# Three steps of a first attention's loop moved between engines and units: the halves of the sums, the weight pieces' rescaling, and the division

## The chip, the cores and the metric

The kernel runs on one core of one Trainium2 chip. A core has five engines that run their own instruction streams and wait for each other by semaphores: TensorE (PE; its weight loads are shown as PEld), VectorE (DVE), ScalarE (ACT), GpSimd (POOL) and SyncE (SP), which here issues all DMAs. The metric is the time of one execution on the device in microseconds; the kernel before has a median of 2089.02 us over 10 runs (2085.13 to 2091.97).

## The reference, cut to what matters

Two layers, each a cross attention, a second mixing stage and a feed-forward part, work on x of 16 batches x 64 tokens x 512 features. The change lies in the first cross attention, over a context of 1601 tokens of 256 features per batch, and in a weight preparation for the last feed-forward part that runs beside it:

```python
qh = (q @ Wq + bq).reshape(B, LQ, HEADS, D_K).transpose(0, 2, 1, 3)   # 16 heads of 32
kh = (k @ Wk + bk)...;  vh = (v @ Wv + bv)...
attn = jax.nn.softmax(jnp.einsum('bhqd,bhkd->bhqk', qh, kh) / np.sqrt(D_K), axis=-1)
out = jnp.einsum('bhqk,bhkd->bhqd', attn, vh)          # then concat @ Wo + bo, added to x
...
s = jnp.maximum(jnp.max(jnp.abs(wb), axis=-1, keepdims=True) / qmax, 1e-12)   # blocks of 32 weights, qmax = 7
wq = jnp.clip(jnp.round(wb / s), -qmax - 1.0, qmax) * s
```

So for each head and query the kernel needs a maximum over the keys, exponentials, their sum, the product with the values, and a division by the sum; and each block of 32 weights of the last feed-forward part is divided by a scale, rounded, and multiplied by the scale again.

## The kernel before, in words

All data are float32. The first attention is a loop over 33 rounds, `for u in range(U + 1)` (L416), with U = 32 units; a unit is one batch and half of the heads (8 heads, 64 queries: 512 columns). Keys lie on partitions, in KC = 13 chunks of 128 (the last has 65). Round u does the first half of unit u (projections of keys and values, scores, running maximum) and the second half of unit u - 1 (subtracting the maximum, exponentials, sums, attention, division). The order within each engine is the order of the text: each instruction of the loop goes through `pin = tc.keep_in_program_order`. DMAs go to SP's queue.

What a round does, with the lines:

- `diagonal(u)` (L273): four POOL copies of the queries into a zeroed tile. For u below 8, POOL also adds a bias to x (L436).
- `next_k` / `k_proj` (L201 by way of `pmm`, L215): keys of unit u, eight pairs of matmuls into the PSUM pool `ps_mm` of two buffers, taken out by ACT. Among them stand `maxima(u - 1)` (L292 transposes `mt`, L294 reduction on DVE) and `shift(u - 1)` (L301 transposes `nb`, L307: seven DVE additions of the negated maximum onto the scores).
- `next_exps` / `exps(u - 1, k)` (L315 on ACT, two chunks at a time). POOL adds the pairs of chunks into `acc`, which has two halves (L320, then L322 four times); with the last, single chunk it adds the second half of `acc` onto the first (L324) and then the last chunk (L325).
- `piece_round(u - 1)` (L169): DVE rounds a piece of weights (L171), POOL multiplies it by its scales (L172), SP stores it (L173). `piece_load(u)` (L156, L160) then loads the next piece. The tiles of a piece (`w`, `wsc`, `winv`) have two buffers.
- `next_v` / `v_proj` (L201, L226): a chunk of values, two matmuls into `ps_mm`, and a DVE addition that takes it out of PSUM; a third chunk needs a buffer that the first one's addition frees. Between them stand `scores(u, 0..2)` (L201; L261 and L265 on ACT) and, on DVE, `running_max(u, k)` (L281, L283, L286).
- In every fourth round (u = 5, 9, ..., 29) `project(g)` (L201, L358) multiplies a finished block of 128 tokens by the output weights; in some rounds a block is normalised and transposed for the next stage.
- The tail: the last two pairs of value chunks before it end, then DVE does `running_max` 4 and 6, `piece_scale(u)` (L164, L165, L166 on DVE, L167 on POOL), `running_max` 8 and 10, two value additions, `running_max` 12, the fold of the two halves of the maximum (L491) and the last value addition. PE meanwhile does `scores(u, 2)`, `attend(u - 1)` (208 matmuls into `av`), `sum_up(u - 1)` (eight matmuls of ones with `acc`) and the value chunks 10, 11, 12. SP issues `load_ctx` in odd rounds (L189).
- `divide(u - 1)` (L349 reciprocal, L350 product, both on DVE, out of the PSUM tile `av`, which has one buffer) ends the round.

Pieces 0 to 30 are prepared in this loop, the other five in the feed-forward stage of the first layer (L768 to L773).

Of the kernel before, what the change touches and what calls it, by code (L numbers as in the profile page):

```python
# [47 lines left out]
def perceiver_kernel(ctx: ExitStack, tc: tile.TileContext, x_d, ctxT_d, ctx_d, cols_d, rows_d,  # L48
# [107 lines left out]
    def piece_load(n, prep):  # L156
        w = prep.tile([P, 16, 32], F32, name="w", tag="wraw")
        raw[n] = (w, prep.tile([P, 16], F32, name="wsc", tag="wsc"),
                  prep.tile([P, 16], F32, name="winv", tag="winv"))
        nc.sync.dma_start(out=w, in_=pieces[n].rearrange("p (b i) -> p b i", b=16))  # L160

    def piece_scale(n, pin=free):
        w, sc, inv = raw[n]
        pin(v.tensor_reduce(sc, w, AX.X, ALU.max, apply_absolute_value=True))  # L164
        pin(v.tensor_scalar(sc, sc, 1.0 / 7.0, 1e-12, ALU.mult, ALU.max))  # L165
        pin(v.reciprocal(inv, sc))  # L166
        pin(gp.tensor_tensor(w, w, inv.unsqueeze(2).to_broadcast([P, 16, 32]), ALU.mult))  # L167

    def piece_round(n, pin=free):  # L169
        w, sc, inv = raw.pop(n)  # L170
        pin(v.tensor_scalar(w, w, RND, RND, ALU.add, ALU.subtract))  # L171
        pin(gp.tensor_tensor(w, w, sc.unsqueeze(2).to_broadcast([P, 16, 32]), ALU.mult))  # L172
        nc.sync.dma_start(out=grid[n], in_=w.rearrange("p b i -> p (b i)"))  # L173

# [3 lines left out]
    with ExitStack() as st1:  # L178
# [117 lines left out]
        def shift(u):  # L296


            nb = ps_mx.tile([P, 4, P], F32, name="nb", tag="mx")
            for j in range(4):  # L300
                pin(pe.transpose(nb[:, j, :], nms[u][:, j:j + 1].to_broadcast([P, P]), ident))  # L301
            nb = nb.rearrange("p j e -> p (j e)")
            f = flat(u)
            for k in range(0, KC, 2):
                n = min(2, KC - k)
                m = nkeys(k + n - 1)
                pin(v.tensor_tensor(f[:m, k:k + n, :], f[:m, k:k + n, :],  # L307
                                    nb[:m].unsqueeze(1).to_broadcast([m, n, 512]), ALU.add))

        def exps(u, k):  # L310

            n = min(2, KC - k)
            m = nkeys(k + n - 1)
            f = flat(u)
            pin(s.activation(f[:m, k:k + n, :], f[:m, k:k + n, :], AF.Exp))  # L315
            if u == 2 * B - 1:
                return
            if k == 2:
                accs[u] = mxp.tile([P, 2, 512], F32, name="acc", tag="acc")
                pin(gp.tensor_tensor(accs[u], f[:, 0:2, :], f[:, 2:4, :], ALU.add))  # L320
            elif 2 < k and n == 2:
                pin(gp.tensor_tensor(accs[u], accs[u], f[:, k:k + 2, :], ALU.add))  # L322
            elif n == 1:
                pin(gp.tensor_tensor(accs[u][:, 0], accs[u][:, 0], accs[u][:, 1], ALU.add))  # L324
                pin(gp.tensor_tensor(accs[u][:m, 0], accs[u][:m, 0], f[:m, k, :], ALU.add))  # L325

        def attend(u, i):
# [18 lines left out]
        def divide(u):  # L346
            b, hf = u // 2, u % 2
            rs = mxp.tile([P, 2, LQ], F32, name="rs", tag="rs")
            pin(v.reciprocal(rs, avs[u][:, 1]))  # L349
            pin(v.tensor_tensor(qo[:, 2 * hf:2 * hf + 2, b * LQ:(b + 1) * LQ], avs[u][:, 0], rs,  # L350
                                ALU.mult))
# [64 lines left out]
        for u in range(U + 1):  # L416
            old, new = u >= 1, u < U
            k_at = iter(range(0, KC, 2))

            def next_exps(n):  # L420
                for _ in range(n if old else 0):
                    exps(u - 1, next(k_at))

            def next_k(i, z):
                if old and new:
                    k_proj(u, i, z)

            def next_v(*ks):
                for k in ks:
                    if old or k >= EARLY:  # L430
                        v_proj(u, k)

            if new:
                diagonal(u)
            if u < G:
                pin(gp.tensor_tensor(x[:, u, :], x[:, u, :], row(R_BO0), ALU.add))  # L436

            normed = [(g, ln_norm(g, pin)) for g in NORM0.get(u, ())]
            next_k(0, 0)
            if old:  # L440
                maxima(u - 1)
            next_k(0, 1)
            if old:
                shift(u - 1)
            next_k(0, 2)
            for g, xn in normed:
                ln_transpose(g, xn, ps_mm, pin)
            next_k(0, 3)
            for z in range(4):
                next_k(1, z)  # L450
                next_exps((1, 1, 0, 2)[z])
            if not new:

                next_exps(3)
                attend(u - 1, 0)
                attend(u - 1, 1)
                sum_up(u - 1, [(flat(u - 1)[:, k, :], nkeys(k)) for k in range(KC)])
                divide(u - 1)
                break
            if old and u <= NPREP:  # L460
                piece_round(u - 1, pin)
            if u < NPREP:
                piece_load(u, prep)
            next_v(0, 1)
            scores(u, 0)
            next_exps(2)
            next_v(2, 3, 4, 5)
            running_max(u, 2)
            if u >= 2 and (u - 2) % 4 == 3:
                g = (u - 2) // 4  # L470
                project(g)
                ln_stats(g, pin)
                if g in (3, 6):
                    ln_scale(0 if g == 3 else 4, g + 1, pin)
            scores(u, 1)
            next_exps(1)
            next_v(6, 7, 8, 9)
            running_max(u, 4)
            running_max(u, 6)
            if u < NPREP:  # L480
                piece_scale(u, pin)
            scores(u, 2)
            if old:
                attend(u - 1, 0)
                attend(u - 1, 1)
                sum_up(u - 1, [(accs[u - 1][:, 0], P)])
            running_max(u, 8)
            running_max(u, 10)
            next_v(10, 11)
            running_max(u, 12)  # L490
            pin(v.tensor_tensor(rms[u][:, 0], rms[u][:, 0], rms[u][:, 1], ALU.max))  # L491
            next_v(12)
            if u % 2 and u // 2 + 2 < B:
                load_ctx(u // 2 + 2)
            if old:
                divide(u - 1)
        project(G - 1)
        ln_stats(G - 1)
        ln_scale(G - 1, G)
# [170 lines left out]
    with ExitStack() as st3:  # L670
# [78 lines left out]
        for q in range(2):  # L749
            t = slice(q * 512, (q + 1) * 512)  # L750
            hT = hp.tile([P, NBLK, 512], F32, name="hT", tag="hT")
            for i in range(NBLK):
                ps = ps3.tile([P, 512], F32, name="ps", tag="mm")
                for c in range(4):
                    mm(ps, w1[:, c, i * P:(i + 1) * P], xnT[:, c, t], c == 0, c == 3)
                s.activation(hT[:, i, :], ps, AF.Relu, bias=col(C_B1 + i))
                v.tensor_tensor(hT[:, i, :], hT[:, i, :], masks[16 * q + i - i % 2][:, i % 2, :],
                                ALU.mult)
                if i % 2:
                    load_mask(16 * q + i + 5)  # L760
                if q and i % 2 == 0 and 2 <= i < 10:
                    ln_out(i // 2 - 1, ps3)
                if not q and i == 1:
                    ln_out(G - 1, ps3)
                    add_rows(row(R_B2))
                if not q and i == 3:
                    route(1)
                if not q and 2 <= i < 2 + len(todo):  # L768
                    piece_load(todo[i - 2], prep)
                if not q and 3 <= i < 3 + len(todo):  # L770
                    piece_scale(todo[i - 3])
                if not q and 4 <= i < 4 + len(todo):
                    piece_round(todo[i - 4])  # L773
            if q:

                ffn0.close()
                ctxa = pool(early, "ctxa4", bufs=2, side="right")
                load_T(0)
            for k in range(4):
                g = 4 * q + k  # L780
                po = ps3.tile([P, 512], F32, name="ps", tag="mm")
                for i in range(NBLK):
                    mm(po, hT[:, i, k * P:(k + 1) * P], w2[:, i, :], i == 0, i == NBLK - 1)
                v.tensor_tensor(x[:, g, :], x[:, g, :], po, ALU.add)
                ln_stats(g)
                if g == 6:
                    ln_scale(4, 7)
            if q == 0:
                ln_scale(0, 4)
# [518 lines left out]
```

## Time and profile before

The profile is of one execution, taken by the hardware profiler.

| what | value |
|---|---|
| median of 10 runs | 2089.02 us |
| the profiled execution's own time | 2084.11 us |
| its span, first to last instruction | 2082.4 us |
| granted TensorE clock over the span | 0.988 |
| first attention's loop, first `av` matmul to last division | 107.6 to 1210.4 us |
| a unit, from one `nb` to the next | 34.6 to 38.4 us |
| busy of the span: PE, DVE, ACT, POOL | 94%, 58%, 38%, 38% |

How to read it: a row of the timeline has the start in us, the duration, the engine, the line, the operation, the tiles it writes and reads, the shapes and the number of instructions merged into the row. In brackets stands the idle time of the engine before it and what ended it. Durations of DVE and POOL contain any time that the instruction itself is held up after its start. The ends of matmuls are modelled.

### The profile page before, as it was taken

To read this page: it belongs to the slowest core of one execution; us is meant where nothing else is said; L and a number is where in the kernel's file an instruction comes from. 1 tells how busy PE (TensorE), PEld (TensorE's weight loads), DVE (VectorE), ACT (ScalarE), POOL (GpSimd) and SP (SyncE) were. 2 spreads that over 40 slices of the span, in tenths; PEclk is the share of its full clock that TensorE was granted. 3 is DMA by queue.
4 is the path that set the end of the run, shared out by engine and by line. 5 is a ranking of instruction groups with operands and counts; after the bars stand their busy time and mean duration, and the time that the engine had idled before them with its cause. 6 is when DMAs were issued, how large, how long until landed. Compare 5 with 4: busy or idle time off the path is not lost. (4 is left out here: it accounts for less than half of the span.)

```text
span 2082.4 us, 38998 instructions
## 1 busy us (share of the span) xinstructions
PE 1960.9 (94%) x17197; PEld 1237.6 (59%) x17197; DVE 1200.5 (58%) x1710; ACT 801.2 (38%) x1112; POOL 781.7 (38%) x494
## 2 busy tenths in 40 slices
PE   8899999999999999999999899899999999999779
PEld 4677677676767677676767654444454555444334
DVE  3577777677676877777676744721113334428751
ACT  2445454444445454544545453210101133316700
POOL 0366667475657566574757521200003000000100
PEclk9999999999999999999999999999999999999889
DMA  5011001101110110111010120520226981200001
GB/s 205 31 44 49 20 39 54 43 22 43 54 43 21 44 48 17 43 54 43 22 43 17 32 102 22 179 66 20 94 73 262 344 313 59 74 0 11 20 0 41
DMA packets 61754, 141.13 MB, mean 68 GB/s; under 512 B 4448, under 2 KB 31600, under 8 KB 60432
## 3 DMA queue, kind: packets, MB, share of 16 engines
q1 hardware_dynamic: 61584, 138.63, 18.6%
q8 instruction: 135, 2.21, 0.4%
q14 instruction: 35, 0.29, 0.0%
HBM read 127.02 MB, written 11.60 MB: 67 GB/s over the span
## 5 line engine op out<-in xcount | busy, mean ns | idle before, releaser
L201 PE MATMUL ps<-wkv,ctxT 128*128 128x256 f32 (+1 forms) x1664 | 399.1, 389 | 15.3 <-DVE vt L226 14.1
L201 PE MATMUL ps<-ctxT,wkv 128*128 128x400 f32 (+1 forms) x1024 | 364.7, 503 | 10.2 <-DMA ctxT<-in_ctxT_dram 8.1
L201 PEld LDWEIGHTS ps<-wkv,ctxT 128*128 128x128 f32 (+1 forms) x1664 | 296.2, 185 | 94.7 <-DVE vt L226 24.8
L226 DVE TENSOR_TENSOR vt<-ps,rows 128x256 f32<-128x256 f32 (+1 forms) x416 | 174.4, 422 | 265.9 <-PE ps L201 264.7
L322 POOL TENSOR_TENSOR acc<-acc,st 128x1024 f32<-128x1024 f32 x124 | 323.6, 2609 | 8.3 <-ACT st L315 1.5
L215 ACT ACTIVATE kt<-ps,cols 128x400 f32<-128x400 f32 (+1 forms) x256 | 152.1, 594 | 365.7 <-PE ps L201 365.7
L261 ACT COPY st<-sc 128x1024 f32<-128x1024 f32 x192 | 185.0, 1016 | 249.9 <-PE sc L201 249.9
L201 PEld LDWEIGHTS ps<-ctxT,wkv 128*128 128x128 f32 x1024 | 189.9, 191 | 138.0 <-issue 9.4
L307 DVE TENSOR_TENSOR st<-st,nb 128x1024 f32<-128x1024 f32 (+1 forms) x224 | 239.1, 1137 | 24.9 <-PE nb L301 24.9
L315 ACT ACTIVATE st<-st 128x1024 f32<-128x1024 f32 (+1 forms) x224 | 215.9, 994 | 10.7 <-DVE st L307 10.3
L283 DVE TENSOR_TENSOR rm<-rm,st 128x1024 f32<-128x1024 f32 x128 | 209.7, 1638 | 2.6
L320 POOL TENSOR_TENSOR acc<-st 128x1024 f32<-128x1024 f32 x31 | 84.8, 2735 | 317.6 <-issue 201.2
L201 PEld LDWEIGHTS sc<-qd,kt 64*128 64x128 f32 x3072 | 179.0, 188 | 36.7 <-issue 32.1
L201 PE MATMUL sc<-qd,kt 64*128 64x128 f32 x3072 | 197.3, 278 | 2.1 <-ACT st L261 2.1
L201 PE MATMUL av<-st,vt 128*32 128x64 f32 x6656 | 109.4, 223 | 23.4 <-issue 18.5
L201 PEld LDWEIGHTS av<-st,vt 128*32 128x32 f32 x6656 | 99.6, 112 | 33.6 <-issue 26.9
L59 PE MATMUL ps<-xnT,w 128*128 128x512 f32 x256 | 112.2, 594 | 0.0
L59 PE MATMUL ps<-w,hT 128*128 128x512 f32 x256 | 110.2, 592 | 0.0
L1192 POOL TENSOR_TENSOR gate<-up,gate 128x1024 f32<-128x1024 f32 x4 | 9.6, 2390 | 259.0 <-ACT up L1191 259.0
L167 POOL TENSOR_TENSOR w<-w,winv 128x512 f32<-128x512 f32 x36 | 65.4, 1819 | 106.5 <-DVE winv L166 96.0
L867 POOL TENSOR_TENSOR xw<-x,wb 128x512 f32<-128x512 f32 x8 | 10.0, 1272 | 210.4 <-ACT wb L860 210.4
L273 POOL COPY qd<-xnT 32x128 f32<-32x128 f32 x128 | 73.4, 574 | 37.5 <-DVE xnT L393 32.4
(236 smaller groups left out, 2358.5 us busy)
## 6 DMA issues: line engine op xcount, KB each, us to landing
cT<-in_ctxT_dram SPq DMA_DIRECT2D x16, 1601.0 KB, 10.3
cN<-in_ctx_dram SPq DMA_DIRECT2D x16, 1536.0 KB, 9.8
ctxT<-in_ctxT_dram SPq DMA_DIRECT2D x15, 1601.0 KB, 6.5
grid<-w SPq DMA_DIRECT2D x36, 256.0 KB, 2.0
w<-grid SPq DMA_DIRECT2D x36, 256.0 KB, 2.7
w<-in_w_dram SPq DMA_DIRECT2D x2, 4096.0 KB
mk<-kept SPq DMA_DIRECT2D x16, 512.0 KB, 4.1
w<-in_wgate_dram SPq DMA_DIRECT2D x12, 256.0 KB, 2.5
```

Source lines behind the costliest of these rows:

```text
L59: pe.matmul(out, lhsT=lhsT, rhs=rhs, start=start, stop=stop)
L167: pin(gp.tensor_tensor(w, w, inv.unsqueeze(2).to_broadcast([P, 16, 32]), ALU.mult))
L201: pin(pe.matmul(out, lhsT=lhsT, rhs=rhs, start=start, stop=stop))
L215: pin(s.activation(kts[u, i][:, o:o + n], ps[:, :n], AF.Identity, bias=col(C_BK0 + c)))
L226: pin(v.tensor_tensor(t[:n, :], ps[:n, :], row(R_BV0 + e, 256)[:n, :], ALU.add))
L261: pin(s.copy(st[:, ks[0]:ks[-1] + 1, r * 256:(r + 1) * 256], sc[:, r]))
L273: pin(gp.tensor_copy(qds[u % 2][r, :, (j % 2) * LQ:(j % 2 + 1) * LQ], qo[r, c:c + 2, b * LQ:(b + 1) * LQ]))
L283: pin(v.tensor_tensor(rms[u], rms[u], f[:, k:k + 2, :], ALU.max))
L307: pin(v.tensor_tensor(f[:m, k:k + n, :], f[:m, k:k + n, :], nb[:m].unsqueeze(1).to_broadcast([m, n, 512]), ALU.add))
L315: pin(s.activation(f[:m, k:k + n, :], f[:m, k:k + n, :], AF.Exp))
L320: pin(gp.tensor_tensor(accs[u], f[:, 0:2, :], f[:, 2:4, :], ALU.add))
L322: pin(gp.tensor_tensor(accs[u], accs[u], f[:, k:k + 2, :], ALU.add))
```

## The change

The sum of the two halves of `acc` leaves POOL (L324) and becomes a DVE addition behind `piece_scale(u)`, after POOL has added the last chunk; `sum_up` then waits for DVE. `piece_round` keeps only the rounding; the product with the scales and the store become `piece_store`, called behind that addition, so that on POOL the product comes after the last of the sums and after `piece_scale`'s product. `piece_load(u)` goes to the start of the round. `divide` of unit u - 2 is done in round u, on DVE behind the shift of unit u - 1, instead of that of unit u - 1 at the end of round u. In the feed-forward stage `piece_store` follows `piece_round` at once, as before.

```diff
     def piece_round(n, pin=free):
+        w = raw[n][0]
+        pin(v.tensor_scalar(w, w, RND, RND, ALU.add, ALU.subtract))
+
+    def piece_store(n, pin=free):
         w, sc, inv = raw.pop(n)
-        pin(v.tensor_scalar(w, w, RND, RND, ALU.add, ALU.subtract))
         pin(gp.tensor_tensor(w, w, sc.unsqueeze(2).to_broadcast([P, 16, 32]), ALU.mult))
         nc.sync.dma_start(out=grid[n], in_=w.rearrange("p b i -> p (b i)"))
...
             elif n == 1:
-                pin(gp.tensor_tensor(accs[u][:, 0], accs[u][:, 0], accs[u][:, 1], ALU.add))
                 pin(gp.tensor_tensor(accs[u][:m, 0], accs[u][:m, 0], f[:m, k, :], ALU.add))
...
+            if u < NPREP:
+                piece_load(u, prep)
             if new:
                 diagonal(u)
...
             if old:
                 shift(u - 1)
+            if u >= 2:
+                divide(u - 2)
             next_k(0, 2)
...
             if old and u <= NPREP:
                 piece_round(u - 1, pin)
-            if u < NPREP:
-                piece_load(u, prep)
             next_v(0, 1)
...
             if u < NPREP:
                 piece_scale(u, pin)
+            if old:
+                acc = accs[u - 1]
+                pin(v.tensor_tensor(acc[:, 0], acc[:, 0], acc[:, 1], ALU.add))
+            if old and u <= NPREP:
+                piece_store(u - 1, pin)
             scores(u, 2)
...
                 load_ctx(u // 2 + 2)
-            if old:
-                divide(u - 1)
         project(G - 1)
...
                     piece_round(todo[i - 4])
+                    piece_store(todo[i - 4])
```

## Prediction

> **What bounds it now.** I read the page's busy shares first, then the busy times by stage, then the waits of the loop, then the timeline of one unit, engine by engine. The page, and the row of the loop from 105 to 1180 us (columns: length; busy time of PE, weight load, DVE, ACT, POOL):
>
> ```profile
> PE 1960.9 (94%) x17197; PEld 1237.6 (59%) x17197; DVE 1200.5 (58%) x1710; ACT 801.2 (38%) x1112; POOL 781.7 (38%) x494
> ```
> ```profile
> 105.00:1180.00 1075.00, 1039.28 (x12443) 767.56 (x12442) 782.54 (x1049) 521.04 (x703) 680.01 (x404) 1.00 0.11 37
> ```
>
> PE is busy 1039.3 of 1075 us, so everything that the change could win in the loop lies in 36 us of PE pauses, a little over 1 us in each of the 31 units that it touches. Which pauses these are, the waits between 100 and 1250 us say (total, times, longest):
>
> ```profile
> PEld ps L201 <- DVE vt L226: 22.4, 29, 1.8
> ...
> PEld nb L301 <- DVE nm L294: 19.9, 31, 1.7
> ...
> PE av L201 <- issue: 19.5, 19, 1.5
> ...
> PE ps L201 <- DVE vt L226: 12.1, 12, 1.4
> ```
>
> Two pauses matter, both at the tail of a unit: PE waits for VectorE's addition of a value chunk (L226, which frees the PSUM buffer), or sits in `av` with no releaser (19 times, about 1 us). The second kind falls inside the attention's matmuls, in one unit between two of the `sum_up` matmuls, long after POOL's last sum; no row names its cause, and I take it to stay. None of these rows names POOL's sums as what PE waits for. One unit's tail, PE, then DVE, then POOL:
>
> ```profile
> 570.15 3.12 PE L201 MATMUL av<-st,vt 128*32 128x64 f32 x208
> 573.09 0.40 PE L201 MATMUL av<-acc,ones 128*32 128x128 f32 x8
> 573.42 1.99 PE L201 MATMUL ps<-wkv,ctxT 128*128 128x256 f32 x8
> 576.62 1.08 PE L201 MATMUL ps<-wkv,ctxT 128*65 128x256 f32 x4 [1.21 <-DVE vt L226]
> ```
> ```profile
> 568.27 1.23 DVE L283 TENSOR_TENSOR rm<-rm,st 128x1024 f32<-128x1024 f32 x1
> 569.53 2.18 DVE L283 TENSOR_TENSOR rm<-rm,st 128x1024 f32<-128x1024 f32 x1
> 571.63 0.68 DVE L164 TENSOR_REDUCE wsc<-w 128x16 f32<-128x512 f32 x1
> 572.35 0.54 DVE L165 TENSOR_SCALAR wsc<-wsc 128x16 f32<-128x16 f32 x1
> 572.92 0.25 DVE L166 RECIPROCAL winv<-wsc 128x16 f32<-128x16 f32 x1
> 573.09 1.16 DVE L283 TENSOR_TENSOR rm<-rm,st 128x1024 f32<-128x1024 f32 x1
> 574.28 1.95 DVE L283 TENSOR_TENSOR rm<-rm,st 128x1024 f32<-128x1024 f32 x1
> 576.15 0.74 DVE L226 TENSOR_TENSOR vt<-ps,rows 128x256 f32<-128x256 f32 x2
> ...
> 578.58 0.94 DVE L349 RECIPROCAL rs<-av 128x128 f32<-128x128 f32 x1
> 579.56 0.29 DVE L350 TENSOR_TENSOR xnT<-av,rs 128x128 f32<-128x128 f32 x1
> ```
> ```profile
> 561.54 1.05 POOL L172 TENSOR_TENSOR w<-w,wsc 128x512 f32<-128x512 f32 x1
> 562.55 5.87 POOL L322 TENSOR_TENSOR acc<-acc,st 128x1024 f32<-128x1024 f32 x2
> 568.50 2.13 POOL L324 TENSOR_TENSOR acc<-acc 128x512 f32<-128x512 f32 x1
> 570.71 2.15 POOL L325 TENSOR_TENSOR acc<-acc,st 65x512 f32<-65x512 f32 x1
> 573.25 1.90 POOL L167 TENSOR_TENSOR w<-w,winv 128x512 f32<-128x512 f32 x1 [0.40 <-DVE winv L166]
> ```
>
> Two things are to be seen. From 568.27 to 576.5 DVE has no pause, and PE's last value chunk (576.62) waits for it: **DVE's tail sets the unit**. And a DVE operation on two SBUF tiles does not run beside a POOL operation. The maximum at 569.53 ends at 571.71, 1.08 us after L324 ends (570.63); L325 ends 1.15 after that maximum; the small L165 takes 0.54 and ends with L325 (572.86), against 0.17 where POOL is idle; L167 ends 0.90 after the maximum of 573.09, the next maximum 1.08 after L167. They alternate, whoever waits being next. So POOL work counts in DVE's tail when it stands there.
>
> **The change, part by part.** Times t are counted from the end of the unit's tenth value addition (568.26 above). By L324 and L325 there are three kinds among the 31 units: 15 like the one above (L324 2.1 us), 9 where POOL is earlier (L324 1.3, L325 2.1; e.g. 425.87), 7 with a projection, where POOL is done before t = 0 (e.g. 532.89, L325 1.26) or L325 comes after exps at -0.1 (two of them). PE's last value chunk starts now at t = 8.36 in the first kind (8.45 in the mean, with the pauses in `av`), 8.56, 7.3 (five) and 7.9 (two).
>
> Removed from POOL ahead of and in the tail: L172 (1.05) and L324 (1.27 alone, 2.13 blocked). In the first kind L322 of the fifth pair then starts at t = -6.6, when its exps (-6.8) are there, and blocks the first maximum to -4.2; that one ends at -3.1, in time for the value addition at -3.0. The sixth pair ends at -0.9, L325 (1.26) at 0.46. The maxima: 0.46 + 1.09 = 1.55, + 1.19 = 2.74; the scale chain (0.68, 0.17, 0.25 with gaps) ends at 3.84 instead of 4.91. In the second kind and the five, L325 is done before 0 and the chain ends at 3.48 (as at 537.85 in the unit that has its t = 0 at 534.37).
>
> Added to the tail: the halves' addition on DVE. The trace has no such row, but the same shape in L491: 0.69; bounds 0.42 (one operand, L171) and 1.65 (L491's longest). I take 0.69, its end at 4.45. It waits for POOL's last sum L325, and behind it on DVE stand the maxima and the value additions that PE waits for; but L325 ends by 2.3 at the latest, and the addition's turn comes at 3.4 to 4.4. `sum_up` needs it at 4.8 (573.09), so PE doesn't wait there. Then, alternating: L167 0.90, maximum 1.08, **L172 0.90**, maximum 1.08: 8.41, and the value addition's end 0.34 later, 8.75; PE starts 0.06 after. L172 is the new guest: bounds 0 (if it slips behind the second maximum) and 1.49 (its longest row); 0.90 is what the alike L167 takes from DVE there.
>
> By kinds: 15 x (8.81 - 8.45) = +5.4. Eight of the 9: 8.46 against 8.56 = -0.8; the ninth, u = 31, has no scale chain: 0. Five projection units: 8.46 - 7.3 = 1.17, +5.8. The two late ones: L325 stays, add and L172 come on top, 1.6 less 0.1: +3.0. Sum **+13.4 us**.
>
> The division leaves the place between the fold of the maxima and their reduction (L349 + L350 = 1.23). What is late next there is PE itself: from `mt` to `nb` the transposes cannot come closer than 1.78 us (578.88 to 580.66), as a projection of keys lies between; over the 31 units the excess over 1.78 is 5.5 us, and that is all it can give: **-5.5 us**. Behind the shift it costs DVE 1.23 us, and then the rounding L171 waits for POOL's first sum (L320, from 553.88, 2.36 alone): the first value addition moves from 555.61 to about 556.6. PE needs its buffer at 558.4; cost nothing. Without that cover it would be up to 1 us a unit, 31 in all. In the last round the division of unit 30 stands before the attention of unit 31 on the one `av` buffer: the attention starts at 1202.5 instead of 1196.85, but its last sixteenths wait for exps until 1202.9 anyway, and the shift starts 0.6 earlier: nothing.
>
> On SP, the store goes to about t = 7.3, lands 2.0 later; the load, which needs that buffer, goes to the unit's start and lands 2.6 later, over 20 us before the scale that reads it. The context's load behind the store waits at t = 9 for PE's last use anyway, and is read two units later. Diagonal copies on POOL slide by about 1 us and are needed 10 us later. All nothing.
>
> Net +13.4 - 5.5 = **+8 us**: 2084.1 (the profiled execution; its span 2082.4) becomes 2092. The runs' median lies 4.9 above that execution, so I forecast 2097.
>
> In the rows the halves' addition takes 1.27 on GpSimd and 0.69 on VectorE. The Trainium skill, GPSIMD Engine Reference, 4.1 Engine selection, says to give elementwise work to VectorE, GpSimd being about twice as slow with two inputs; by it alone this move saves 0.58 x 31 = 18 us, but the rows show the faster engine to be the one that PE waits for. Against the new place of L172 speaks SBUF — State Buffer, section "SBUF: two separate sides": the shared port pair is held for a whole instruction while the other engine blocks; with L172's whole 1.05 instead of 0.90 the sum would be some 4.5 us higher.
>
> **Rivals.** (a) *The tail gets shorter*: L172 doesn't come between the two last maxima. Then every tail ends 0.95 earlier than above: PE would start at 7.9 or 7.5, but where `av` has its 1 us pause not before 8.2. Pause-free units gain 0.45 (4) and 1.05 (5), the paused ones 0.2 (11) and 0.3 (3), five projection units lose 0.25, the two 0.6: -7.7, and -5.5 from the division: -13, **2076**. The sign of the forecast turns where a tail costs 8 / 31 = 0.26 us less than taken. For it: POOL starts 0.08 us behind its releaser (573.25 after 573.17), DVE 0.03 behind its own last one. Against: a waiting L167 was always next. (b) *It cancels*: the first kind becomes like the second (L325 done by t = 0), 0.36 less in 15 units, -5: +3, **2092**. This is also what follows if the pause of `av` already hides the added part. (c) *Slower by more*: the pauses in `av` move behind the wait. They lie under the wait for DVE now; where they fall after the last value chunk, 15 units pay 1.1 again: +8 + 16 = **2113**. It decides from the point where whatever PE lacks there is asked for later than the last chunk, t = 8.8; the pause sits at t = 3 to 6 now, against it. (d) *It doesn't do what it says*, since the addition waits for POOL after all: it would need L325 to end after 3.8, and its latest end is 2.3.
>
> **Chances.** Forecast 0.45 (own range 2089 to 2106), (a) 0.20, (b) 0.20, (c) 0.13, (d) with the rest 0.02. What this kernel's measurement can tell from no change is about 0.2%, 4.2 us: faster 0.20, same 0.25, slower 0.55. The range takes in (b), nearly all of (a) and most of (c): 2077 to 2112.
>
> **What would show it.** In the profile after: L172 between the two last L283 of a tail, each some 1.95 long; the addition 0.7 long directly behind L166; the wait of `ps` for `vt` grown from 1.2 to about 1.6 us in plain units and newly there in projection units; `nb` 1.78 after `mt` in all units. Wrong, if L172 lies behind the last maximum, if PE waits in `sum_up` for DVE, or if the first value chunk of a unit makes PE wait.

## The result, and the profile after

The changed kernel takes 2094.96 us in the median of 14 runs (2090.71 to 2099.64), against 2087.21 us for the kernel before in the runs beside it: ratio 1.0036, 95% interval 1.0027 to 1.0046, 7.7 us slower. The forecast was 8 us slower (2097 us, with a range of 2077 to 2112). The profiled execution took 2090.71 us, its span 2089.0.

The row of the loop from 105 to 1180 us (length; busy time of PE, weight load, DVE, ACT, POOL), and its waits, both of the kernel after:

```profile
105.00:1180.00 1075.00, 1032.26 (x12428) 766.53 (x12426) 842.45 (x1077) 518.60 (x700) 608.85 (x372) 1.00 0.11 37
```
```profile
PEld ps L204 <- DVE vt L229: 35.3, 30, 2.0
...
PE ps L204 <- DVE vt L229: 23.3, 24, 1.6
DVE nm L297 <- PE mt L295: 22.5, 30, 0.9
PE av L204 <- issue: 19.4, 19, 1.8
```

POOL has lost 71 us of work and DVE has gained 60; PE, the busiest engine, is busy 7 us less in the same stretch. PE's wait for the value addition has grown from 12.1 to 23.3 us (22.4 to 35.3 at the weight load). The pauses in `av` are as they were (19.5, 19.4). The weight load's wait of `nb` for `nm` has fallen from 19.9 us in 31 places to 1.0 us in one; DVE now waits for the transposes `mt` instead. One plain unit (without a projection), PE, then DVE, then POOL (lines have moved: L201 is L204, L226 L229, L283 L286, L322 L325, L325 L327, L172 L175; L488 is the new addition). In the text the lines of the kernel before are meant, unless a row beside it shows others:

```profile
574.05 0.40 PE L204 MATMUL av<-acc,ones 128*32 128x128 f32 x8
...
577.95 1.08 PE L204 MATMUL ps<-wkv,ctxT 128*65 128x256 f32 x4 [1.57 <-DVE vt L229]
```
```profile
572.79 0.25 DVE L166 RECIPROCAL winv<-wsc 128x16 f32<-128x16 f32 x1
572.96 0.63 DVE L488 TENSOR_TENSOR acc<-acc 128x512 f32<-128x512 f32 x1
573.51 2.06 DVE L286 TENSOR_TENSOR rm<-rm,st 128x1024 f32<-128x1024 f32 x1
575.61 1.95 DVE L286 TENSOR_TENSOR rm<-rm,st 128x1024 f32<-128x1024 f32 x1
577.48 0.74 DVE L229 TENSOR_TENSOR vt<-ps,rows 128x256 f32<-128x256 f32 x2
```
```profile
568.35 1.26 POOL L327 TENSOR_TENSOR acc<-acc,st 65x512 f32<-65x512 f32 x1
573.13 1.36 POOL L167 TENSOR_TENSOR w<-w,winv 128x512 f32<-128x512 f32 x1 [3.51 <-DVE winv L166]
574.45 2.02 POOL L175 TENSOR_TENSOR w<-w,wsc 128x512 f32<-128x512 f32 x1
```

This unit has its t = 0 at 569.23. The scale chain (L164 to L166) ends at t = 3.82 (4.91 before), the addition at 4.36. Then the turns alternate as laid out: L167 ends at 574.49, 0.90 after the addition; the maximum at 575.57, 1.08 later; L175 at 576.47, 0.90 later; the second maximum at 577.56, 1.09 later. These four steps are 0.90, 1.08, 0.90 to 0.91 and 1.08 us in all 30 units with a scale chain. PE's last value chunk starts at t = 8.72 instead of 8.36.

### The profile page after: what moved, and what is told of

It is laid out like the page before. It is cut to its first block, busy times and chain, and to the rows that moved or that the text cites. A ratio compares the mean times of both kernels' runs of the same rounds, so it can differ in the third digit from the quotient of the medians.

```text
span 2089.0 us, 39026 instructions
## 1 busy us (share of the span) xinstructions
PE 1956.6 (94%) x17197; PEld 1237.4 (59%) x17197; DVE 1262.5 (60%) x1741; ACT 801.3 (38%) x1112; POOL 712.3 (34%) x463
## 5 line engine op out<-in xcount | busy, mean ns | idle before, releaser
L204 PE MATMUL ps<-wkv,ctxT 128*128 128x256 f32 (+1 forms) x1664 | 401.8, 390 | 26.6 <-DVE vt L229 25.2
L204 PE MATMUL ps<-ctxT,wkv 128*128 128x400 f32 (+1 forms) x1024 | 364.6, 503 | 10.2 <-DMA ctxT<-in_ctxT_dram 8.1
L204 PEld LDWEIGHTS ps<-wkv,ctxT 128*128 128x128 f32 (+1 forms) x1664 | 297.2, 186 | 107.6 <-DVE vt L229 37.7
L325 POOL TENSOR_TENSOR acc<-acc,st 128x1024 f32<-128x1024 f32 x124 | 319.3, 2575 | 23.6 <-ACT st L318 18.6
L229 DVE TENSOR_TENSOR vt<-ps,rows 128x256 f32<-128x256 f32 (+1 forms) x416 | 170.3, 419 | 185.5 <-PE ps L204 185.3
L204 PEld LDWEIGHTS ps<-ctxT,wkv 128*128 128x128 f32 x1024 | 189.9, 191 | 137.8 <-issue 9.3
L318 ACT ACTIVATE st<-st 128x1024 f32<-128x1024 f32 (+1 forms) x224 | 216.0, 994 | 12.2 <-DVE st L310 11.8
L286 DVE TENSOR_TENSOR rm<-rm,st 128x1024 f32<-128x1024 f32 x128 | 214.8, 1678 | 2.2
L204 PEld LDWEIGHTS sc<-qd,kt 64*128 64x128 f32 x3072 | 178.9, 188 | 36.8 <-issue 24.5
L204 PE MATMUL sc<-qd,kt 64*128 64x128 f32 x3072 | 197.3, 278 | 2.1 <-ACT st L264 2.1
L323 POOL TENSOR_TENSOR acc<-st 128x1024 f32<-128x1024 f32 x31 | 73.4, 2367 | 311.3 <-issue 193.4
L204 PE MATMUL av<-st,vt 128*32 128x64 f32 x6656 | 107.5, 222 | 27.1 <-issue 18.2
L204 PEld LDWEIGHTS av<-st,vt 128*32 128x32 f32 x6656 | 99.3, 112 | 35.8 <-issue 26.6
L167 POOL TENSOR_TENSOR w<-w,winv 128x512 f32<-128x512 f32 x36 | 48.4, 1347 | 163.5 <-DVE winv L166 152.8
L276 POOL COPY qd<-xnT 32x128 f32<-32x128 f32 x128 | 78.8, 615 | 37.3 <-DVE xnT L395 32.3
L59 PE MATMUL po<-wdT,gate 128*128 128x512 f32 x192 | 84.4, 603 | 3.2 <-DVE gate L1222 3.2
```

The costliest lines, as they stand in the source:

```text
L59: pe.matmul(out, lhsT=lhsT, rhs=rhs, start=start, stop=stop)
L204: pin(pe.matmul(out, lhsT=lhsT, rhs=rhs, start=start, stop=stop))
L229: pin(v.tensor_tensor(t[:n, :], ps[:n, :], row(R_BV0 + e, 256)[:n, :], ALU.add))
L276: pin(gp.tensor_copy(qds[u % 2][r, :, (j % 2) * LQ:(j % 2 + 1) * LQ], qo[r, c:c + 2, b * LQ:(b + 1) * LQ]))
L286: pin(v.tensor_tensor(rms[u], rms[u], f[:, k:k + 2, :], ALU.max))
```

## The experiments

The numbers of one profiled execution each, in the order of the table: the time from t = 0 of unit 1 to the start of the last division (the loop); the start of the last value chunk in a plain unit without a pause in `av` and in the projection unit u = 21; the sum of what `nb` comes later than 1.78 us after `mt`, units 1 to 30.

| kernel | ratio to before (95%) | loop, us | chunk, plain | chunk, u = 21 | excess of nb, us |
|---|---|---|---|---|---|
| before | 1 | 1103.3 | 8.36 or 8.56 | 7.17 | 5.2 |
| before, second profile | | 1104.6 | 8.36 or 8.56 | 7.13 | 5.6 |
| after | 1.0036 (1.0027 to 1.0046) | 1110.8 | 8.72 | 8.38 | 0.0 |
| after, second profile | | 1109.3 | 8.72 | 8.39 | 0.0 |
| e1, division alone | 0.9979 (0.9966 to 0.9992) | 1103.6 | 8.57 | 7.13 | 0.1 |
| e2, product and store alone | 0.9946 (0.9926 to 0.9965) | 1096.9 | 8.24 | 7.13 | 5.8 |
| e3, addition alone | 1.0030 (1.0017 to 1.0044) | 1113.8 | 8.33 or 8.71 | 7.66 | 5.5 |
| e4, addition ahead of the scale | 0.9932 (0.9916 to 0.9947) | 1094.0 | 7.86 | 7.54 | 0.0 |
| e5, e4 with the last round mended | 0.9932 (0.9910 to 0.9953) | 1092.3 | 7.86 | 7.53 | 0.0 |
| e6, halves summed on TensorE | 0.9952 (0.9931 to 0.9973) | 1092.1 | 7.27 | 7.85 (paused) | 0.2 |
| e7, product not moved | 1.0015 (0.9999 to 1.0031) | 1104.7 | 8.33 | 7.66 | 0.4 |
| e8, division not moved | 1.0061 (1.0042 to 1.0079) | 1110.8 | 8.74 | 8.39 | 2.5 |
| e9, addition not moved | 0.9927 (0.9906 to 0.9949) | 1090.2 | 8.23 | 7.28 | 0.0 |

From the start of the last division to the end of the span the thirteen profiled executions took 870 to 882 us, though the code there is the same. So the loop and its rows are read from the traces, and the totals from the ratios. The two do not agree in size everywhere: e2 is 11 us faster by its ratio and 6 to 8 by its loop. That part stays open.

**The theory** is that of the prediction: in the tail of a unit VectorE and GpSimd take turns, and the loss is made by the addition, which puts L167 and L172 one turn ahead of the maxima that PE waits for. **The rivals**: the addition's (or the product's) own duration costs, wherever it stands; or the division's new place costs.

### The three parts alone

e1, the division alone:

```diff
+            if u >= 2:
+                divide(u - 2)          # behind shift(u - 1)
...
-            if old:
-                divide(u - 1)          # end of the round
```

> The kernel before with the division alone moved behind the next unit's shift. Turn-taking (the loss of the whole change is made in the DVE tail by L172's turn and the addition): the tail is untouched, the last value chunk keeps t = 8.4 and 8.6, the excess of mt to nb over 1.78 us goes (-5.9 us in the trace of the whole change), the last round's attention waits for the division of unit 30 (+2.5 us): 3 us faster than before, ratio 0.998 to 0.999. Rival (the division's new place is what costs, through the first value addition and the last round): slower by 3 to 8 us.

Measured 0.9979 (0.9966 to 0.9992), 4 us faster: the division's new place does not cost, and that rival falls. The excess of `nb` goes from 5.2 to 0.1 us, as expected, and the last round pays 2.5 us. But in the loop of this execution the gain is eaten up: the chunk stands at 8.57 in all plain units (8.36 or 8.56 before), and from `nb` to the next tail 15 units take 0.2 us more each. Where that comes from, DVE's and POOL's rows of e1 ahead of a tail show:

```profile
556.99 1.27 DVE L171 TENSOR_SCALAR w<-w 128x512 f32<-128x512 f32 x1
...
564.27 3.08 DVE L281 TENSOR_TENSOR rm<-st 128x1024 f32<-128x1024 f32 x1
567.28 0.41 DVE L226 TENSOR_TENSOR vt<-ps,rows 128x256 f32<-128x256 f32 x1
```
```profile
562.92 1.05 POOL L172 TENSOR_TENSOR w<-w,wsc 128x512 f32<-128x512 f32 x1
563.92 5.65 POOL L322 TENSOR_TENSOR acc<-acc,st 128x1024 f32<-128x1024 f32 x2
```

The rounding behind the division takes 1.27 instead of 0.42 us, for POOL has begun its first sum, and the first two value additions slide; from the third on they are back in their place (13.57 us after `nb`, 13.62 before). The changed kernel shows the same (1.26, 13.57) and loses nothing by it. What costs is the first maximum (L281): L172, in its old place, lets POOL's next sum start only 0.35 us ahead of it, and it takes 3.08 us instead of 1.22 before and 2.54 in the changed kernel. The seventh value addition is then 0.3 us later than in the changed kernel. The same place is late in e7, which also moves the division and leaves L172, and not in e9, which moves both. The loops are thus equal (1103.6 against 1103.3 and 1104.6) while the ratio says 4 us; what makes the difference I can't name.

e2, product, store and load alone:

```diff
             if u < NPREP:
                 piece_scale(u, pin)
+            if old and u <= NPREP:
+                piece_store(u - 1, pin)
```

(with `piece_round` split and `piece_load` at the start of the round, as in the change.)

> The kernel before with the product with the scales and the store moved behind piece_scale, and the load at the round's start, alone. Turn-taking: without the addition in front, VectorE's maximum comes first, then L167, then the second maximum, and L172 only after it, so that the tail doesn't pay for it; in the units where POOL is early L325 ends 1 us sooner: last value chunk 8.36 in plain units as before, 7.9 to 8.3 instead of 8.56 in the early kind: 2 to 5 us faster, ratio 0.998 to 0.999. Rival (each part costs by itself, L172's 0.9 us stand in every tail): 0.9 us in some 20 tails, slower by 10 to 20 us.

Measured 0.9946 (0.9926 to 0.9965), 11 us faster, more than expected. POOL and DVE of e2, a unit with its t = 0 at 566.67:

```profile
571.54 1.90 POOL L167 TENSOR_TENSOR w<-w,winv 128x512 f32<-128x512 f32 x1 [2.25 <-DVE winv L166]
573.40 2.02 POOL L175 TENSOR_TENSOR w<-w,wsc 128x512 f32<-128x512 f32 x1
```
```profile
572.58 1.95 DVE L286 TENSOR_TENSOR rm<-rm,st 128x1024 f32<-128x1024 f32 x1
574.45 0.74 DVE L229 TENSOR_TENSOR vt<-ps,rows 128x256 f32<-128x256 f32 x2
```

L175 starts as early as in the changed kernel relative to L167, but the second maximum ends at 574.53, 1.09 us after L167 (573.44), and L175 only 0.89 later (575.42), while DVE does value additions out of PSUM (0.74 for two, as in the kernel before). The product in its new place costs the chunk nothing here, and its absence further up makes the sums end sooner (L325 at t = 2.6; before, 2.9 or 4.6). The rival (0.9 us in each tail) falls.

e3, the addition alone:

```diff
-                pin(gp.tensor_tensor(accs[u][:, 0], accs[u][:, 0], accs[u][:, 1], ALU.add))
...
                 piece_scale(u, pin)
+            if old:
+                acc = accs[u - 1]
+                pin(v.tensor_tensor(acc[:, 0], acc[:, 0], acc[:, 1], ALU.add))
```

> The kernel before with the halves' addition alone moved to VectorE behind piece_scale; L172 and the division stay. Turn-taking: the addition puts L167's turn ahead of the first maximum and one diagonal copy (0.15 us) ahead of the second; last value chunk about 8.75 in plain units (8.36 before), 8.3 in the early kind, 7.75 with a projection: slower by 4 to 9 us, ratio 1.002 to 1.004. Rival (the parts simply add up): as the other two parts alone gain about 3 us each by turn-taking's own numbers, this one would have to cost 13 us for the whole change's 8, ratio 1.006.

Measured 1.0030 (1.0017 to 1.0044): slower by itself, in the expected size, and half of what the parts would need to add up. The three ratios sum to 2.1 + 5.4 - 3.0 = 4.5 thousandths faster; the whole is 3.6 slower. So the addition loses by itself, but **most of what turns the gain into a loss, 8.1 thousandths, lies in the meeting of the parts**: the chunk in a projection unit stands at 7.13 with the product alone, at 7.66 with the addition alone, and at 8.38 with both (7.17 with none): 0.5 us expected by adding up, 1.2 measured, and the 0.7 between is L172's turn (0.90), which stands where e3 has one diagonal copy (0.15 us by the expectation). In the loops of the single profiles the same sum is less clear (+0.3 - 6.4 + 10.5 = +4.4 against +7.4), because e3's loop has a loss of its own: in units 1, 2 and 6 POOL's bias addition now stops the fold of the maxima (1.64 instead of 0.69), in unit 3 the maximum ahead of it (1.65), 0.8 to 1.4 us each.

### Each part taken out of the whole

e7 puts product, store and load back; e8 puts the division back; both keep the other two parts.

```diff
# e7
+                piece_store(u - 1, pin)       # behind piece_round(u - 1), piece_load behind it
...
-                piece_store(u - 1, pin)       # behind the addition
# e8
-                divide(u - 2)                 # behind the shift
...
+                divide(u - 1)                 # end of the round
```

> The changed kernel with product, store and load back at their old places: the addition behind piece_scale and the division a unit later remain. If L172's turn in the tail is part of the loss: last value chunk as in the kernel with the addition alone (8.3 or 8.7 in plain units, 7.7 with a projection) instead of 8.72 and 8.38, so 6 to 10 us faster than the changed kernel, ratio to before 0.998 to 1.001. Rival (the addition alone makes the loss): as the changed kernel, 1.003 to 1.004.

Measured 1.0015 (0.9999 to 1.0031), 5 us less than the changed kernel: the chunk falls to 8.33 and 7.66 as expected, the loop by 4.6 to 6.1 us. L172's turn in the tail is part of the loss, the addition keeps the rest. The gain is a little below the 6 to 10 us expected; the late seventh value addition told at e1 comes back here.

> The changed kernel with the division back at the end of the round: addition and product stay moved. Theory: the excess of nb over 1.78 us behind mt comes back in the 20 or so units (+5.9 us), and the last round's wait for the division goes (-2.5 us): 2 to 5 us slower than the changed kernel, ratio to before 1.004 to 1.006. Rival (the division's new place costs more than it gives): faster than the changed kernel, ratio 1.001 to 1.003.

Measured 1.0061 (1.0042 to 1.0079), 5 us more than the changed kernel, as expected (the two intervals still touch), and again without the loop of one execution showing it (1110.8 against 1110.8 and 1109.3): of the excess only 2.5 us come back, in the normalising units, and the last round's 2.3 us go; unit 31 is 1.5 us shorter as well, since the first profile of the changed kernel has a halved clock there (below). By the ratios the division is worth having in either surrounding; its size by the rows stays open.

### Other orders of the same work

e4 changes nothing but the place of the addition:

```diff
+            if old:
+                acc = accs[u - 1]
+                pin(v.tensor_tensor(acc[:, 0], acc[:, 0], acc[:, 1], ALU.add))
             if u < NPREP:
                 piece_scale(u, pin)
-            if old:
-                acc = accs[u - 1]
-                pin(v.tensor_tensor(acc[:, 0], acc[:, 0], acc[:, 1], ALU.add))
```

> The changed kernel with the addition put ahead of piece_scale(u) instead of behind it; everything else as changed. Same work on the same engines, other order. Turn-taking: the maximum follows the reciprocal at once again, L167 comes after the first maximum and L172 after the second, so a turn of 0.9 us leaves the tail: last value chunk at about 7.9 in plain units, 7.6 with a projection, 8.3 to 8.6 where the pause in av stands; 12 to 18 us faster than the changed kernel, that is 4 to 10 us faster than before, ratio 0.995 to 0.998. Rival (the addition's 0.69 us on VectorE and L172's 0.9 us cost wherever they stand before the second maximum): as the changed kernel, ratio 1.003 to 1.004.

Measured 0.9932 (0.9916 to 0.9947): the same instructions as the changed kernel on the same engines, 1.04% faster than it by the two ratios, and faster than the 0.995 to 0.998 expected; its loop is 15 to 17 us shorter, within the 12 to 18 expected. This is the experiment that decides. PE, DVE and POOL of e4 (t = 0 at 564.12):

```profile
571.99 1.08 PE L204 MATMUL ps<-wkv,ctxT 128*65 128x256 f32 x4 [0.71 <-DVE vt L229]
```
```profile
566.76 0.69 DVE L486 TENSOR_TENSOR acc<-acc 128x512 f32<-128x512 f32 x1
...
568.46 3.14 DVE L286 TENSOR_TENSOR rm<-rm,st 128x1024 f32<-128x1024 f32 x2
571.52 0.74 DVE L229 TENSOR_TENSOR vt<-ps,rows 128x256 f32<-128x256 f32 x2
```
```profile
568.62 1.90 POOL L167 TENSOR_TENSOR w<-w,winv 128x512 f32<-128x512 f32 x1 [4.12 <-DVE winv L166]
570.48 2.02 POOL L175 TENSOR_TENSOR w<-w,wsc 128x512 f32<-128x512 f32 x1
```

The addition takes its 0.69 us here as well. But the maximum follows the reciprocal at once, L167 waits for it, the second maximum waits for L167 (568.62 + 1.90 = 570.52) and ends at 571.60, and L175 ends at 572.50, behind it. The chunk starts at t = 7.86 instead of 8.72: 0.86 less, one turn. The rival that the operations' own time is the loss would have left it at 8.72.

e5 puts, in the last round alone, the division of unit 30 ahead of the shift:

```diff
+            if not new:
+                divide(u - 2)
             if old:
                 shift(u - 1)
-            if u >= 2:
+            if u >= 2 and new:
                 divide(u - 2)
```

> The kernel with the addition ahead of piece_scale, and in the last round the division of unit 30 put ahead of the shift of unit 31 instead of behind it. Theory: the last round's attention waits only for the av buffer that this division frees (8.9 us of pause in the changed kernel, its sums 2.5 us later than before); ahead of the shift the attention starts with the first exponentials again: 2 to 3 us faster than without, ratio to before 0.991 to 0.993. Rival (the last exponentials end the round anyway, as forecast): the same time as without, or slower by the division's 1.2 us ahead of the shift, ratio 0.993 to 0.994.

The ratio is the same as e4's (0.9932, 0.9910 to 0.9953), so the times do not tell. A gain of 2 to 3 us is smaller than the intervals. The rows do, in part: from `nb` to the first matmul of the last sums it is 12.57 us instead of 15.01, and the loop is 1.7 us shorter, though both executions have one long pause with a halved clock behind it (below; e4 in unit 7, e5 in unit 31).

e6 leaves the addition out and lets TensorE sum both halves (the result is the same sum):

```diff
-                sum_up(u - 1, [(accs[u - 1][:, 0], P)])
+                sum_up(u - 1, [(accs[u - 1][:, 0], P), (accs[u - 1][:, 1], P)])
```

> The kernel with the last round mended and no addition of the halves at all: TensorE sums both halves, eight more matmuls of ones in a unit (0.4 us by the row of the eight there are); piece_scale, the products, the store and the division as in the changed kernel. If VectorE's tail is what bounds a unit everywhere: last value chunk at about 7.3 to 7.5 in all units, 0.5 us less than with the addition ahead of the scale, 10 to 15 us faster than that kernel, ratio 0.986 to 0.988. If in the 15 to 18 units with a pause in av it is TensorE by now: those get 0.35 us longer (+5 us), the others 0.3 shorter (-3 us): ratio 0.992 to 0.995.

Measured 0.9952 (0.9931 to 0.9973), the second case, at its upper end. PE of e6, a unit with a pause:

```profile
430.05 0.81 PE L204 MATMUL av<-st,vt 128*32 128x64 f32 x43 [0.89 <-issue]
...
431.29 2.86 PE L204 MATMUL ps<-wkv,ctxT 128*128 128x256 f32 x12
```

All twelve value matmuls run in one piece: PE no longer waits for DVE here. Where no pause stands the chunk starts at 7.27, where one stands at 7.8 to 9.1. With the tail shortened the pause bounds the unit, and the eight more matmuls make it later: with a pause of 1.1 us the chunk starts at about 8.6, against 8.4 in e5.

e9 leaves the addition on POOL, with product and division moved and the last round mended:

```diff
+                pin(gp.tensor_tensor(accs[u][:, 0], accs[u][:, 0], accs[u][:, 1], ALU.add))   # POOL, ahead of the last chunk
...
-                pin(v.tensor_tensor(acc[:, 0], acc[:, 0], acc[:, 1], ALU.add))
```

> The changed kernel without the addition on VectorE: POOL adds the halves where it did (ahead of the last chunk); product, store and load, and the division as changed, the last round's division ahead of the shift. If the two moves that gained alone (division 0.9979, product 0.9946) don't disturb each other: last value chunk at 8.2 as with the product alone, mt to nb 1.78 us everywhere, ratio to before 0.991 to 0.994, as fast as with the addition ahead of the scale. If the addition on VectorE is needed for a gain: 0.996 to 0.998.

Measured 0.9927 (0.9906 to 0.9949), median 2071.11 us: as expected, as fast as e4 and e5 within their intervals, and the shortest loop (1090.2). The addition on VectorE isn't needed for the gain. Both e4 and e9 beat the two kernels of this case.

### The profiles taken again

> The kernel before, profiled a second time, to see how far one profiled execution speaks for the others. Theory: the value chunk's place in a plain unit without a pause in av (8.36 and 8.56) and the excess of nb are the same to 0.05 us, and the time from unit 1's tail to the last division is 1103 us to within 3 us; what differs between executions lies in the pauses in av and behind the loop.

The places are the same to 0.02 us in the plain units without a pause (which unit is of which kind differs), the excess 5.6 against 5.2, the loop 1104.6. The execution took 2086.24 us.

> The changed kernel, profiled a second time, for the same reason. Theory: 8.72 and 8.38 in the tails as before; unit 31's 1.8 us pause in av with the halved clock behind it, and so 2 us of its loop, need not come again: 1107 to 1111 us from unit 1's tail to the last division.

The chunk at 8.72 and 8.39, the loop 1109.3; unit 31's chunk at 8.92 instead of 10.36. The execution took 2095.43 us.

## Why the prediction was right, step by step

- **What bounds a unit.** Right. DVE's tail sets it, by POOL's turns; seven of the eight orders tried above put the chunk of plain units within 0.12 us of what the turns say. e1 is the miss: every plain unit became of the later kind (8.57). In e6 the tail is so short that TensorE's pause sets the units that have one.
- **The turns in the plain units.** Right: 8.81 and 8.46 were worked out for the two kinds, 8.72 measured for both, because L325 ends at t = 0.38 in all of them, not at 0.46 in one kind and before 0 in the other. Over the 23 of them with a scale chain +5.1 us (forecast +4.6). The chunk stands at 8.72 with a pause in `av` and without, so the pauses did not move behind the wait, as rival (c) had it.
- **L172 as the new guest** at 0.90 us between the two maxima: right, 0.90 by its row. The rule of the Trainium skill that spoke against its place (SBUF — State Buffer, "SBUF: two separate sides": the pair is held for the whole instruction) agrees with the alternation; a waiting product took 0.90 us of DVE's time here, not the 1.05 of its row alone.
- **The projection units**: +5.4 for the five (forecast +5.8), +2.8 for the two late ones (+3.0).
- **Unit 31**, forecast 0: +2.1 in one pair of profiles, +0.4 in the other. It isn't the turns: PE's last chunk doesn't wait for DVE there. The pause in `av` was longer, 1.80 instead of 1.02 us with a halved clock behind it in the first pair, 1.69 instead of 1.30 in the second.
- **The division's excess**: -5.9 with unit 31 (forecast -5.5). Its new place at "cost nothing" held in the changed kernel: no unit takes longer from `nb` to the next tail. With L172 in its old place it costs 0.2 us in some units, as e1 and e7 show.
- **The last round**, "nothing": wrong. The last exponentials were taken to end it, but with 8.85 us of idle time ahead all 208 matmuls of the attention come after the division, and they take 5.38 us. Before, 80 of them were done while the exponentials still ran, and only 128 were left. PE, before and after:

```profile
1202.44 3.66 PE L201 MATMUL av<-st,vt 128*32 128x64 f32 x128 [0.42 <-ACT st L315]
1205.93 3.02 PE L201 MATMUL av<-st,ones 128*32 128x128 f32 x104
```
```profile
1207.72 5.38 PE L204 MATMUL av<-st,vt 128*32 128x64 f32 x208 [8.85 <-DVE xnT L352]
1212.91 3.03 PE L204 MATMUL av<-st,ones 128*32 128x128 f32 x104
```

From `nb` to the first matmul of the sums it is 14.7 us instead of 12.2: +2.5 (14.0 instead of 12.7, +1.4, in the second pair). The granted clock is halved for 10 to 14 us of this round in every profile, before the change too.
- **Not seen at all**: gains of 0.8 and 0.7 us in units 4 and 5, where POOL's bias addition L436 had stopped the fold (L491's 1.65) and now comes after it, and 3.9 us between `nb` and the next tail (2.7 in the second pair), most of it in the normalising units and three others. They made good for the last round and unit 31. So the mechanism and the large terms were right, but that the total is right to 0.5 us is luck: terms put at nothing or not seen came to 4 to 5 us on either side. The loop in the two pairs of profiles grew by 7.4 and 4.7 us. The forecast median, 2097, is 2 us above the measured one, nearly all of it because the median of the kernel before was 2089.02 when the forecast was made and 2087.21 beside the changed kernel.
- **The rival (a)**, that L172 does not come between the maxima, did not happen in this change, but it is what e2, e4 and e9 do on purpose.
- **The rule to give elementwise work to VectorE** (the Trainium skill, GPSIMD Engine Reference, 4.1 Engine selection): the addition is indeed 0.63 to 0.69 us there against 1.27, and it made the kernel slower alone (1.0030) and no faster in the better of the two places tried (e5, 0.9932, against e9, 0.9927, with the addition on GpSimd).

## What to carry to other kernels

Where VectorE and GpSimd block each other, as here, look at the order of the next few operations on both, and not at their durations alone: list who waits when each one ends, and put an operation where the other engine isn't waiting for a turn. Here the same instructions in another order were 1.04% faster. Test the parts of a change alone and together: here two parts that gain turned into a loss through a third. In a loop that is moved by one round, look at the last round by itself.

## What the runs showed of the hardware that I had not expected

The pauses in `av` go with instruction transfers. The page counts these on the instruction queue:

```profile
q8 instruction: 135, 2.21, 0.4%
```

These are 135 transfers of 16 KB. In the profiles of before and after, two of each, all 74 pauses of over 0.2 us in the attention ahead of the last round end 1.2 to 1.6 us after such a transfer has ended; there is one about every 128 pairs of weight load and matmul, and the attention's 208 pairs pass in 3 us. Most transfers pass without such a pause: 98 end in the loop of before, which has 19 pauses. The distance is nearly the same in every case; that the transfer releases the pause is the plain reading, though no run changed it by itself. In e6, with 16 more instructions in a unit, the pauses fell in other units.

Behind some of these pauses the granted clock fell to half for 3.4 us. PE of e4, and the clock of the stretch from 320 to 324 us (the third number from the end: 0.83):

```profile
321.14 0.25 PE L204 MATMUL av<-st,vt 65*32 65x64 f32 x3 [1.71 <-issue]
...
321.60 4.53 PE L204 MATMUL ps<-wkv,ctxT 128*128 128x256 f32 x12
```
```profile
320.00:324.00 4.00, 2.86 (x21) 2.30 (x21) 2.34 (x2) 0.00 (x0) 3.84 (x6) 0.83 0.08 30
```

The twelve matmuls take 4.53 us instead of 2.86. It came behind pauses of 1.71 (e4), 1.80 (after, unit 31) and 1.80 us (e5), not behind one of 1.75 (e7) nor behind the waits of 1.56 to 1.62 that the changed kernel has in its units without a pause (10 in this profile). Two waits of PE for VectorE were longer still, 1.92 us in e8 and 1.84 in the second profile of the changed kernel (unit 29 in both), and no halved clock followed. So the length of the pause alone doesn't decide; what does is not shown.
